# First depthwise tap folded into the projection weights, a third DMA product in every band, and a new order of work

## The chip, the cores and the metric

The kernel runs on one core of one Trainium2 chip. The metric is device time in microseconds of a whole execution, as the median of several runs. The profile covers one execution, from the first to the last instruction of the program (the span); the time of a run is some 20 us more than that.

Five engines run side by side and wait for each other only through semaphores: PE (matmuls), DVE (vector), ACT (activations and copies), POOL (GpSimd, which here also issues the adding DMAs) and SP (which issues plain DMAs). Sixteen DMA engines move data.

## The reference

The input x has 16 images of 128 channels, 96 x 96 pixels, in float32. One Restormer-like block is computed:

```python
x_hwc = x.transpose(0, 2, 3, 1)
xn1 = _layernorm(x_hwc, ln1_w, ln1_b)
x = x + _attention(xn1, wq, wk, wv, wp).transpose(0, 3, 1, 2)
xn2 = _layernorm(x.transpose(0, 2, 3, 1), ln2_w, ln2_b).transpose(0, 3, 1, 2)
h1 = einsum('bchw,oc->bohw', xn2, w_in)                 # 128 -> 512 channels
h2 = depthwise 3x3 convolution of h1 with w_dw, padding 1
h3 = gelu(h2)
x = x + einsum('bchw,oc->bohw', h3, w_out)              # 512 -> 128 channels
```

The attention is over channels (8 heads of 16), so that it needs one 128 x 128 Gram matrix per image. The change concerns the last four lines: the projection w_in, the nine taps of the depthwise convolution, the gelu and the projection back.

## The kernel before

**Tiling.** An image is 8 bands of 12 rows (1152 pixels); 16 images make 128 bands, called g. A band is 3 units of 4 rows (384 pixels). The 512 hidden channels are 4 chunks of 128, called n. A conv job is one chunk of one band, (g, n).

**Stages.** For each image `norm(i, False)` transposes x by PE (line 581), takes statistics on DVE (588), variance and power on POOL (595, 599), scales on ACT (626), forms the Gram matrix (640), transposes back (671) and copies to the padded buffer xn (677). `attention` makes one 128 x 128 matrix from the Gram matrix. `norm(i, True)` multiplies by that matrix (539), adds x (by a DMA that adds, 551) and normalizes again, into xn (675, 681).

**A conv job** (`conv_job`, line 838). PE multiplies by winT (line 856) and ACT copies the result from PSUM to h1 (861), with two rows kept from the band before (`halo`, 852). Then the nine taps are summed in h3, a buffer of 128 x 1152. Tap t is h1, shifted by t, times the channel's weight `dw[:, n, t]`. There are three ways for a tap:

- Tap 0 is a product on ACT that starts h3 (line 872 with h3 as the output).
- Taps 1 and 2 are products on ACT into buffers called pr (line 872 with pr as the output); a DMA adds the second to the first (line 880, pr<-pr), and another adds the first to h3 (line 880, h<-pr). In chunk 1 of two bands out of three (`THIRD`, line 26) tap 3 goes this way also. POOL issues these adding DMAs.
- The other taps are one DVE instruction each, h3 = h1 shifted x weight + h3 (line 876).

When all are in, ACT applies gelu to h3 in place (884), and `ffn_out` multiplies by woutT on PE (950), adds to x on DVE (957) and stores the band by SP (961).

In 66 of the 128 bands chunk 3 takes another way (`by_matmuls`, line 915): the weights of w_in and of each tap are multiplied together beforehand (`comp`), and nine matmuls per unit accumulate in PSUM (927); ACT applies gelu from there (933). So there are 446 conv jobs.

**What sets the order.** The kernel lists its operations with an engine, an assumed duration, a place and what it reads and writes (`Plan.op`, line 66). `Plan.order` (line 96) walks through assumed time; each free engine takes the ready operation with the lowest place. A place is the number of the job that it belongs to plus an offset per kind of operation, from the table `AT` (line 32). Buffers of some pools (`IN_TURN`) are given out in the order of place. The result is one fixed list for each engine. At run time an engine works through its own list in order and stalls at the first instruction whose inputs are not there. There are 10 h3 buffers, 5 pr buffers and 4 PSUM banks for the matmuls of this stage.

The weights are prepared once at the start (`weights`, line 401): they are transposed by PE and scaled by the second norm's weight w2 on the way out of PSUM.

Of the kernel before, what the change touches and what calls it, by code (L numbers as in the profile page):

```python
# [9 lines left out]
F32 = mybir.dt.float32  # L10
AF = mybir.ActivationFunctionType
ALU = mybir.AluOpType
# [6 lines left out]
BR = 12  # L19
# [2 lines left out]
PE_OF = 2  # L22
PE_LAST = (0, 1, 2, 4, 5, 7)
TINY = 1e-20
DMA_TAPS = (1, 2, 3)
THIRD, THIRD_OF, THIRD_CHUNK = (0, 1), 3, 1
PART, Z_PARTS = 24, 6
QT, QB = 4, 1
H_BANKS = 4
X1_BUFS, XB_BUFS, PR_BUFS, H3_BUFS, ZT_BUFS = 2, 6, 5, 10, 3  # L30
IN_TURN = ("tr", "h3", "pr", "xb", "x1")
AT = dict(
    weights=8.1, zeros=0.25, load_a=-21.3, forth_a=-15.05, stats_a=-18, variance_a=-18.05, power_a=-1.8,
    scaled_a=0.55, gram=-6.85, back_a=-25.85, place_a=-18.35, attention=-17.8, mix=-10.5, residual=4.7,
    mixed=-4.65, add_x=14, forth_b=-14.75, stats_b=-10.65, variance_b=-15.9, power_b=-13.85,
    shift_b=-25.75, scaled_b=3.95, back_b=-24.6, place_b=5.05, halo=9.05, hidden=0.85, kept=-0.9,
    product=-13.2, products=5.45, add_last=-13.7, tap=3.45, add_first=27.05, gelu=-5.15, conv=0.55,
    conv_gelu=-14.15, out=4.35, add=-4.2, store=7.05,
)
STEP = dict(scaled=0.3, hidden=0.1, products=0.5, tap=0.166, conv=1.6, conv_tap=0.03, out=0.8, out_part=0.05)  # L40
SLACK = 300
# [9 lines left out]
class Plan:  # L51
# [14 lines left out]
    def op(self, engine, ns, place, work, reads, writes, result, own=None, dma=0, two=False):  # L66

        k = len(self.ops)
        needs = {}
        for t in reads:
            if t in self.writer:
                needs[self.writer[t]] = True
        for t in writes:
            if t in self.writer:
                needs[self.writer[t]] = True
            for r in self.readers.get(t, ()):  # L80
                needs[r] = True
        for t in reads:
            self.readers.setdefault(t, []).append(k)
        new = []
        for t in writes:
            self.writer[t], self.readers[t] = k, []
            if t[0] in self.free and t[:2] not in self.users and t[:2] not in new:
                new.append(t[:2])
        for t in {t[:2]: None for t in (*reads, *writes)}:
            if t[0] in self.free:  # L90
                self.users.setdefault(t, []).append(k)
                needs[self.users[t][0]] = True
        needs.pop(k, None)
        self.ops.append((engine, ns, place, work, list(needs), new, result, own or result, dma, two))
# [111 lines left out]
def tile_restormer_block(  # L206
# [24 lines left out]
    nc = tc.nc  # L231
    B, C, H, W = x.shape
    P = 128
    HID = w_in.shape[0]
    NCH = HID // P
# [42 lines left out]
    wv_sb = const.tile([P, P], F32, name="wv_sb")  # L278
    nc.scalar.dma_start(out=wv_sb, in_=wv)
    dw = const.tile([P, NCH, 9], F32, name="dw")  # L280
    nc.scalar.dma_start(out=dw, in_=w_dw.rearrange("(n p) o kh kw -> p n (o kh kw)", p=P))

    wvb = const.tile([P, 1], F32, name="wvb")
# [59 lines left out]
    def at(kind, place):  # L343
        return place + AT[kind]
# [16 lines left out]
    def t_act(n, scalars=0):  # L361
        return 95 + 93 * scalars + 0.832 * n
# [7 lines left out]
    def dve(ns, p, f, r, w, two=False):  # L370
        op("DVE", ns, p, f, r, w, ns + 120 + SLACK, ns + 120, two=two)
# [7 lines left out]
    def act(ns, p, f, r, w):  # L379
        op("ACT", ns, p, f, r, w, ns + 150 + SLACK, ns + 150)  # L380
# [20 lines left out]
    def weights(p):  # L401
# [17 lines left out]
        def transposed(parts, kept, gives):  # L419

            key = ("weights", next(names))
            h = ("h", key)
            d = {}

            def forth():
                d["pt"] = bank(key)
                for k, part in enumerate(parts()):
                    nc.tensor.transpose(d["pt"][:, k * P : (k + 1) * P], part, ident)

            pe(440, at("weights", p), forth, mine, [h])  # L430
            dve(700, at("weights", p), lambda: kept(d["pt"]), [h], [("w", g) for g in gives] + mine[1:])
# [37 lines left out]
        def shifts():  # L469
# [4 lines left out]
            nc.vector.reciprocal(none, w2)  # L474
            nc.vector.tensor_mul(b2, b2, none)

        op("ACT", 400, at("load_a", p), loads, [], mine, T_WEIGHTS, dma=2 * T_MOVE)
        dve(400, at("weights", p), shifts, [], [("w", "in"), ("w", "conv"), ("w", "shift")])
        transposed(
            lambda: [v["wqk"][:, :P], v["wqk"][:, P:], v["wp"], wv_sb], keep_qkp, ["qk"]  # L480
# [3 lines left out]
        pc = ("h", ("weights", "centred"))  # L484
        pe(1000, at("weights", p), centred, [("w", "qk"), mine[1]], [pc])
        dve(800, at("weights", p), keep_centred, [pc], [("w", "qk")])
        transposed(
            lambda: [v["win"][:, n, :] for n in range(NCH)],
            lambda pt: nc.vector.tensor_scalar(winT.rearrange("p n c -> p (n c)"), pt, w2, None, ALU.mult), ["in"],
        )  # L490
        transposed(
# [341 lines left out]
    def h3_of(g, n):  # L833
        if (g, n) not in h3s:
            h3s[g, n] = h3p.tile([P, BR, W], F32, tag="h3", name=f"h3_{g}_{n}")
        return h3s[g, n]

    def conv_job(j, g, n):

        i, b = divmod(g, NB)  # L840
        kz, r0 = part_of(i, b * BR)
        xn = xns[kz]
        d = {}
        jn = (g, n)
        from_halo = n != PE_CHUNK and b > 0
        to_halo = n != PE_CHUNK and b < NB - 1
        h1_ = h1s[n]
        step = 4 if from_halo else 5
        chunks = [(k, min(k + step, BR + 2)) for k in range(2 if from_halo else 0, BR + 2, step)]

        def halo():
            nc.scalar.copy(window(h1_, 0, 2, 1), window(h1_, BR, 2, 1))

        def hidden(r, e):
            ph = d["ph", r] = bank((jn, r), (e - r) * W)
            nc.tensor.matmul(  # L856
                rows(ph), lhsT=winT[:, n, :], rhs=window(xn, r0 + r, e - r, 1), start=True, stop=True
            )

        def kept(r, e):  # L860
            nc.scalar.copy(window(h1_, r, e - r, 1), rows(d.pop(("ph", r))))  # L861

        def shifted(t):
            dy, dx = divmod(t, 3)
            return window(h1_, dy, BR, dx)

        def product(t):
            if t == 0:
                to = h3_of(g, n)
            else:  # L870
                to = d["pr", t] = prp.tile([P, BR, W], F32, tag="pr", name=f"pr_{g}_{n}_{t}")
            nc.scalar.activation(to, shifted(t), AF.Copy, scale=dw[:, n, t : t + 1])  # L872

        def tap(t):
            h3 = h3_of(g, n)
            nc.vector.scalar_tensor_tensor(h3, shifted(t), dw[:, n, t : t + 1], h3, ALU.mult, ALU.add)  # L876

        def add_products(t):
            to = d["pr", DMA_TAPS[0]] if t != DMA_TAPS[0] else h3_of(g, n)
            nc.gpsimd.dma_start(out=to, in_=d["pr", t], accum_op=ALU.add)  # L880

        def gelu(s0, s1):
            h3 = h3_of(g, n)[:, s0 * UR : s1 * UR, :]
            nc.scalar.activation(h3, h3, AF.Gelu)  # L884

        last = j == len(jobs) - 1
        third = n == THIRD_CHUNK and g % THIRD_OF in THIRD
        dma_taps = () if last else DMA_TAPS[: 3 if third else 2]
        left = [t for t in range(1, 9) if t not in dma_taps]
        h1 = [("h1", n, k) for k in range(4)]  # L890
        h3 = [("h3", jn, s) for s in range(UPB)]
        for k, (r, e) in enumerate(chunks):
            ph = ("h", (jn, r))
            jk, zs = j + STEP["hidden"] * k, z_units(kz, r0 + r, r0 + e)
            to = h1[k + 1 : k + 2] if r else h1[:2]
            pe(t_mm((e - r) * W), at("hidden", jk), lambda r=r, e=e: hidden(r, e), [*zs, ("w", "in")], [ph])
            act(t_copy((e - r) * W), at("kept", jk), lambda r=r, e=e: kept(r, e), [ph], to)
        act(t_act(BR * W, 1), at("product", j), lambda: product(0), h1, h3)
        for k, t in enumerate(dma_taps):
            jk = j + STEP["products"] * k  # L900
            act(t_act(BR * W, 1), at("products", jk), lambda t=t: product(t), h1, [("pr", (jn, t))])
        pr = [("pr", (jn, t)) for t in dma_taps]
        for k, t in enumerate(dma_taps[1:]):
            add(at("add_last", j), lambda t=t: add_products(t), [pr[1 + k]], [pr[0]])
        for k, t in enumerate(left):
            dve(t_dve(BR * W), at("tap", j + STEP["tap"] * k), lambda t=t: tap(t), h1, h3, True)
        if dma_taps:
            add(at("add_first", j), lambda: add_products(DMA_TAPS[0]), [pr[0]], h3)
        if to_halo:
            act(t_copy(2 * W), at("halo", j), halo, h1[3:], h1[:1])  # L910
        for s in range(0, UPB, 1 if last else UPB):
            e = s + 1 if last else UPB
            act(t_act((e - s) * UT), at("gelu", j), lambda s=s, e=e: gelu(s, e), [], h3[s:e])
# [121 lines left out]
```

## Time and profile before

| | before |
|---|---|
| time, median of 3 | 4262.72 us (4255.91 to 4265.92) |
| span of the profile | 4242.3 us |
| instructions | 52552 |
| POOL busy | 2403.9 us (57%) |
| DMA bytes | 802.87 MB, mean 189 GB/s |
| adds pr<-pr, h<-pr, to x (issues; us to landing) | 531; 6.8, 445; 7.0, 122; 7.5 |

A line of a group reads: line, engine, operation, output<-inputs, shape, count, then busy time in us and mean ns of one, then the engine's idle time just before them and what ended most of it. A record of an instruction can overlap the next one on the same engine, so that the busy time of a group (the time in which at least one of its instructions ran) can be below count times mean. PEld is the loading of weights into the PE, which overlaps matmuls. A matmul in float32 is two instructions.

Queue rows of the page, in words: the queue of adding DMAs (software_dynamic) moved 647.70 MB and took 80.5% of the time of the 16 DMA engines; the plain loads and stores (hardware_dynamic) moved 151.01 MB and took 9.8%.

### The profile page before, as it was taken

The numbers are of one execution on the slowest core, as the hardware profiler recorded it, in microseconds if no ns is written. First come the engines' busy times: TensorE is split into PE (matmuls) and PEld (weight loads), VectorE is DVE, ScalarE is ACT, GpSimd is POOL, SyncE is SP. The second block draws the span as 40 slices with busy tenths as digits, with TensorE's granted clock in tenths as the row PEclk, the third lists the DMA queues.
The fourth block names the chain that finished last, engine by engine and source line by source line (L and its number), as shares of the span: only waits on it lengthen the run. The fifth ranks groups of instructions, "written<-read, shape, count | busy, mean of one in ns | idle before, by whom it ended". The sixth has DMA issues, their size and how long they took to land.

```text
span 4242.3 us, 52552 instructions
## 1 busy us (share of the span) xinstructions
PE 4175.6 (98%) x17457; PEld 2667.1 (63%) x17457; DVE 4121.0 (97%) x4705; ACT 4080.1 (96%) x7374; POOL 2403.9 (57%) x2331
## 2 busy tenths in 40 slices
PE   8999999999999999999999999999999999999999
PEld 6566666666665666666666666666666666666565
DVE  6999999999999999999999999999999999999999
ACT  5999999999999999999999999999999999999996
POOL 4656556565665656655656565666655556465432
PEclk9999999999999999999999999999999999999999
DMA  2989899899998999899999989999989899998997
GB/s 81 188 179 203 187 199 205 187 203 189 192 193 188 195 192 198 186 191 199 191 207 190 194 190 185 204 191 193 207 179 202 188 198 198 182 201 180 185 188 161
DMA packets 197887, 802.87 MB, mean 189 GB/s; under 512 B 22896, under 2 KB 24304, under 8 KB 197616
## 3 DMA queue, kind: packets, MB, share of 16 engines
q0 software_dynamic: 158112, 647.70, 80.5%
q1 hardware_dynamic: 37152, 151.01, 9.8%
q8 instruction: 138, 2.26, 0.2%
q10 hardware_dynamic: 2352, 0.81, 0.1%
q14 instruction: 133, 1.09, 0.1%
HBM read 148.26 MB, written 75.50 MB: 53 GB/s over the span
## 4 chain that ended last, share of the span: by engine, by line
PE 49%; ACT 20%; DVE 13%; DMA 5%; issue 3%; POOL 1%; POOLq 0%; ACTq 0%; DVEq 0%
PE h L927 15%; PE h L950 11%; DVE h L876 11%; PE h L856 10%; ACT pr L872 5%; DMA h<-pr 3%; PE g L640 3%; PE h L539 3%; ACT h L861 3%; ACT h L884 2%; ACT h L872 2%; ACT zT L630 2%; PE pB_a L671 2%; PE pT_b L581 1%; PE pB_b L671 1%
## 5 line engine op out<-in xcount | busy, mean ns | idle before, releaser
L876 DVE SCALAR_TENSOR_TENSOR h<-h,dw,h 128x1152 f32<-128x1152 f32 x2592 | 3563.1, 1410 | 12.6 <-ACT h L872 9.3
L872 ACT ACTIVATE pr<-h,dw 128x1152 f32<-128x1152 f32 x976 | 1319.9, 1376 | 8.9 <-DMA pr<-pr 8.8
L927 PE MATMUL h<-xn,comp 128*128 128x384 f32 x3564 | 1268.1, 486 | 4.3 <-ACT h L861 2.6
L950 PE MATMUL h<-h,woutT 128*128 128x384 f32 x3072 | 1120.9, 488 | 12.2 <-ACT h L861 7.2
L856 PE MATMUL h<-xn,winT 128*128 128x384 f32 (+1 forms) x2676 | 1055.2, 501 | 10.7 <-ACT h L861 3.7
L927 PEld LDWEIGHTS h<-xn,comp 128*128 128x128 f32 x3564 | 648.1, 190 | 402.6 <-issue 14.1
L880 POOL DMA_DIRECT2D pr<-pr x531 | 493.0, 934 | 596.1 <-ACT pr L872 444.5
L950 PEld LDWEIGHTS h<-h,woutT 128*128 128x128 f32 x3072 | 558.2, 190 | 366.0 <-ACT h L861 17.5
L861 ACT COPY h<-h 128x384 f32<-128x384 f32 (+1 forms) x1338 | 722.2, 605 | 21.2 <-PE h L856 18.7
L880 POOL DMA_DIRECT2D h<-pr x445 | 425.2, 963 | 520.6 <-DVE h L876 183.2
L856 PEld LDWEIGHTS h<-xn,winT 128*128 128x128 f32 x2676 | 483.1, 190 | 320.6 <-issue 38.9
L872 ACT ACTIVATE h<-h,dw 128x1152 f32<-128x1152 f32 x446 | 603.8, 1361 | 1.8 <-PE h L950 0.2
L884 ACT ACTIVATE h<-h 128x1152 f32<-128x1152 f32 x448 | 565.7, 1263 | 34.4 <-DMA h<-pr 32.1
L599 POOL TENSOR_TENSOR rstd_b<-ve_b,mhalf 128x4 f32<-128x4 f32 x288 | 496.6, 1730 | 10.4
L599 POOL TENSOR_TENSOR rstd_a<-ve_a,mhalf 128x4 f32<-128x4 f32 x288 | 492.8, 1712 | 10.5 <-POOL ve_a L595 0.2
L630 ACT ACTIVATE zT<-pT_b,nb_b,rstd_b 128x128 f32<-128x128 f32 x1132 | 455.9, 572 | 4.5 <-DVE nb_b L603 4.5
L595 POOL TENSOR_SCALAR ve_b<-st_b 128x4 f32<-128x4 f32 x288 | 297.3, 1041 | 257.0 <-DVE st_b L588 253.9
L595 POOL TENSOR_SCALAR ve_a<-st_a 128x4 f32<-128x4 f32 x288 | 275.8, 958 | 265.7 <-DVE st_a L588 263.6
L626 ACT ACTIVATE zT<-pT_a,rstd_a 128x128 f32<-128x128 f32 x1080 | 339.3, 492 | 13.6 <-POOL rstd_a L599 13.4
L640 PE MATMUL g<-zT 128*128 128x129 f32 x2304 | 306.7, 276 | 0.0
L539 PE MATMUL h<-xn,mwT 128*128 128x384 f32 x768 | 284.0, 489 | 2.1 <-ACT zT L630 0.7
L640 PEld LDWEIGHTS g<-zT 128*128 128x128 f32 x2304 | 282.4, 192 | 2.5 <-issue 0.4
(165 smaller groups left out, 3713.2 us busy)
## 6 DMA issues: line engine op xcount, KB each, us to landing
pr<-pr POOLq DMA_DIRECT2D x531, 576.0 KB, 6.8
h<-pr POOLq DMA_DIRECT2D x445, 576.0 KB, 7.0
x<-in_x_dram SPq DMA_DIRECT2D x128, 576.0 KB, 6.2
out_dram<-x SPq DMA_DIRECT2D x127, 576.0 KB, 5.3
x<-in_x_dram POOLq DMA_DIRECT2D x122, 576.0 KB, 7.5
out_dram<-x SPq DMA_DIRECT2D x3, 192.0 KB, 1.9
weights<-in_L_conv_w_in_dram ACTq DMA_DIRECT2D x1, 256.0 KB, 11.3
weights<-in_L_conv_w_out_dram ACTq DMA_DIRECT2D x1, 256.0 KB, 12.2
```

The costliest lines, as they stand in the source:

```text
L595: nc.gpsimd.tensor_scalar(ve, d["mv"][:, :, 2], 1.0 / C, EPS, ALU.mult, ALU.add)
L599: nc.gpsimd.tensor_tensor(rstd, d["ve"], mhalf, ALU.pow)
L630: nc.scalar.activation(zT(q)[:, k, :P], d["pT", q][:, k, :], AF.Identity, bias=d["nb"][:, t : t + 1], scale=d["rstd"][:, t : t + 1],)
L640: nc.tensor.matmul(grams[i][:, : P + 1], lhsT=zt[:, :P], rhs=zt, start=(q == 0 and k == 0), stop=(q == NU * TPU // QT - 1 and k == QT - 1),)
L856: nc.tensor.matmul(rows(ph), lhsT=winT[:, n, :], rhs=window(xn, r0 + r, e - r, 1), start=True, stop=True)
L861: nc.scalar.copy(window(h1_, r, e - r, 1), rows(d.pop(("ph", r))))
L872: nc.scalar.activation(to, shifted(t), AF.Copy, scale=dw[:, n, t : t + 1])
L876: nc.vector.scalar_tensor_tensor(h3, shifted(t), dw[:, n, t : t + 1], h3, ALU.mult, ALU.add)
L880: nc.gpsimd.dma_start(out=to, in_=d["pr", t], accum_op=ALU.add)
L884: nc.scalar.activation(h3, h3, AF.Gelu)
L927: nc.tensor.matmul(d["pc"], lhsT=comp[:, t, :], rhs=window(xn, r0 + dy, UR, dx), start=(t == 0), stop=(t == 8),)
L950: nc.tensor.matmul(rows(d["po"]), lhsT=woutT[:, n, :], rhs=h3s[g, n][:, s * UR : (s + 1) * UR, :], start=(k == 0), stop=(k == NCH - 1),)
```

## The change

It has three parts.

1. **Tap 0's weight goes into the projection.** Before it is transposed, w_in is multiplied by tap 0's weight of each hidden channel (`unit`; a weight that is almost zero is replaced by a tiny one). Then h1 shifted is tap 0's product, and no instruction is needed for it. The other taps use `ratio`, their weight divided by tap 0's. The first tap on DVE reads h1 twice, once with its own shift and weight, once with shift 0, and writes h3.
2. **The third DMA product in chunk 1 of every band.** `THIRD` takes all three residues of g instead of two.
3. **A new table `AT`**, and so a new order on every engine.

```diff
+UNIT_MIN = 1e-18
-THIRD, THIRD_OF, THIRD_CHUNK = (0, 1), 3, 1
+THIRD, THIRD_OF, THIRD_CHUNK = (0, 1, 2), 3, 1
...
 AT = dict(
-    weights=8.1, zeros=0.25, load_a=-21.3, forth_a=-15.05, stats_a=-18, variance_a=-18.05, power_a=-1.8,
...
-    product=-13.2, products=5.45, add_last=-13.7, tap=3.45, add_first=27.05, gelu=-5.15, conv=0.55,
-    conv_gelu=-14.15, out=4.35, add=-4.2, store=7.05,
+    weights=86, zeros=34, load_a=-17.95, forth_a=-1.35, stats_a=-23.85, variance_a=50.15, power_a=-16.45,
...
+    scaled_b=98.5, back_b=-23.15, place_b=20.55, halo=21.65, hidden=1.35, kept=-79.55, products=8.4,
+    add_last=-64.4, tap=0.1, add_first=-14.5, gelu=-63.5, conv=1.15, conv_gelu=-1.85, out=4.9, add=-43.45,
+    store=47.1,
 )
...
+        def units():
+
+            w0 = dw[:, :, 0]
+            nc.vector.tensor_scalar(unit, w0, -1.0, None, ALU.mult)
+            nc.vector.tensor_tensor(unit, unit, w0, ALU.max)
+            nc.vector.tensor_scalar(unit, unit, UNIT_MIN, 3 * UNIT_MIN, ALU.is_lt, ALU.mult)
+            nc.vector.tensor_add(unit, unit, w0)
+            nc.vector.reciprocal(per_unit, unit)
+            for n in range(NCH):
+                nc.vector.tensor_scalar(ratio[:, n, :], dw[:, n, :], per_unit[:, n : n + 1], None, ALU.mult)
+
+        def unit_parts():
+            for n in range(NCH):
+                nc.vector.tensor_scalar(v["wt"][:, n, :], v["win"][:, n, :], unit[:, n : n + 1], None, ALU.mult)
...
         def product(t):
-            if t == 0:
-                to = h3_of(g, n)
-            else:
-                to = d["pr", t] = prp.tile([P, BR, W], F32, tag="pr", name=f"pr_{g}_{n}_{t}")
-            nc.scalar.activation(to, shifted(t), AF.Copy, scale=dw[:, n, t : t + 1])
+            to = d["pr", t] = prp.tile([P, BR, W], F32, tag="pr", name=f"pr_{g}_{n}_{t}")
+            nc.scalar.activation(to, shifted(t), AF.Copy, scale=ratio[:, n, t : t + 1])
 
         def tap(t):
             h3 = h3_of(g, n)
-            nc.vector.scalar_tensor_tensor(h3, shifted(t), dw[:, n, t : t + 1], h3, ALU.mult, ALU.add)
+            onto = shifted(0) if t == left[0] else h3
+            nc.vector.scalar_tensor_tensor(h3, shifted(t), ratio[:, n, t : t + 1], onto, ALU.mult, ALU.add)
...
-        act(t_act(BR * W, 1), at("product", j), lambda: product(0), h1, h3)
```

In `weights` the transposes of w_in read the multiplied copy `wt` in place of `win`, with `units` and `unit_parts` listed on DVE before them.

More of the change, by code (lines that the diff above doesn't have):

```diff
@@ L32 @@
 AT = dict(
-    weights=8.1, zeros=0.25, load_a=-21.3, forth_a=-15.05, stats_a=-18, variance_a=-18.05, power_a=-1.8,
-    scaled_a=0.55, gram=-6.85, back_a=-25.85, place_a=-18.35, attention=-17.8, mix=-10.5, residual=4.7,
-    mixed=-4.65, add_x=14, forth_b=-14.75, stats_b=-10.65, variance_b=-15.9, power_b=-13.85,
-    shift_b=-25.75, scaled_b=3.95, back_b=-24.6, place_b=5.05, halo=9.05, hidden=0.85, kept=-0.9,
-    product=-13.2, products=5.45, add_last=-13.7, tap=3.45, add_first=27.05, gelu=-5.15, conv=0.55,
-    conv_gelu=-14.15, out=4.35, add=-4.2, store=7.05,
+    weights=86, zeros=34, load_a=-17.95, forth_a=-1.35, stats_a=-23.85, variance_a=50.15, power_a=-16.45,
+    scaled_a=6.1, gram=-31.8, back_a=-145.85, place_a=68, attention=-19.55, mix=-17.6, residual=60.15,
+    mixed=-98.2, add_x=-22.85, forth_b=-2, stats_b=-5.55, variance_b=52.05, power_b=-11, shift_b=-76.95,
+    scaled_b=98.5, back_b=-23.15, place_b=20.55, halo=21.65, hidden=1.35, kept=-79.55, products=8.4,
+    add_last=-64.4, tap=0.1, add_first=-14.5, gelu=-63.5, conv=1.15, conv_gelu=-1.85, out=4.9, add=-43.45,
+    store=47.1,
 )
@@ L280, in tile_restormer_block @@
     dw = const.tile([P, NCH, 9], F32, name="dw")
+    ratio = const.tile([P, NCH, 9], F32, name="ratio")
+    unit = const.tile([P, NCH], F32, name="unit")
+    per_unit = const.tile([P, NCH], F32, name="per_unit")
     nc.scalar.dma_start(out=dw, in_=w_dw.rearrange("(n p) o kh kw -> p n (o kh kw)", p=P))
@@ L475, in shifts @@
             nc.vector.tensor_mul(b2, b2, none)
+        def units():
[10 more added lines that the diff above has]
+                nc.vector.tensor_scalar(v["wt"][:, n, :], v["win"][:, n, :], unit[:, n : n + 1], None, ALU.mult)
         op("ACT", 400, at("load_a", p), loads, [], mine, T_WEIGHTS, dma=2 * T_MOVE)
+        dve(1400, at("weights", p), units, [], [("w", "in")])
         dve(400, at("weights", p), shifts, [], [("w", "in"), ("w", "conv"), ("w", "shift")])
@@ L486, in weights @@
         dve(800, at("weights", p), keep_centred, [pc], [("w", "qk")])
+        dve(700, at("weights", p), unit_parts, [mine[0], ("w", "in")], [mine[1]])
         transposed(
-            lambda: [v["win"][:, n, :] for n in range(NCH)],
+            lambda: [v["wt"][:, n, :] for n in range(NCH)],
             lambda pt: nc.vector.tensor_scalar(winT.rearrange("p n c -> p (n c)"), pt, w2, None, ALU.mult), ["in"],
```

## The prediction

> **What bounds the kernel now.** I read the page's first part (busy time per engine) and then its slices:
>
> ```profile
> PE 4175.6 (98%) x17457; PEld 2667.1 (63%) x17457; DVE 4121.0 (97%) x4705; ACT 4080.1 (96%) x7374; POOL 2403.9 (57%) x2331
> ...
> DVE  6999999999999999999999999999999999999999
> ACT  5999999999999999999999999999999999999996
> ...
> DMA  2989899899998999899999989999989899998997
> ```
>
> Three engines are full at once, from the first tenth to the end. No stage has a single bound, so a saving on one engine alone need not show. The windows view (per stretch: length, then busy time and count for PE, PEld, DVE, ACT, POOL, then clock, DMA share, GB/s) gives start, middle and end:
>
> ```profile
> 0.00:106.00 106.00, 87.72 (x546) 69.72 (x547) 66.39 (x183) 53.21 (x134) 43.61 (x100) 0.95 0.27 81
> 106.00:4136.00 4030.00, 3985.46 (x16592) 2537.70 (x16591) 3958.57 (x4441) 3957.40 (x7146) 2338.61 (x2207) 1.00 0.93 193
> 4136.00:4243.00 107.00, 102.43 (x324) 59.70 (x322) 96.06 (x83) 69.51 (x97) 21.67 (x24) 1.00 0.76 160
> ```
>
> In the middle, 4030 us, DVE and ACT are both 98.2% busy and the DMA engines 0.93. The PE's 3985 us needs care, since matmuls overlap in the records. The timeline gives the true spacing:
>
> ```profile
> 2008.43 1.06 PE L640 MATMUL g<-zT 128*128 128x129 f32 x8
> ...
> 2009.66 0.81 PE L856 MATMUL h<-xn,winT 128*128 128x384 f32 x2
> ...
> 2013.86 0.60 PE L581 MATMUL pT_b<-ident,x 128*128 128x128 f32 x4
> ...
> 2020.47 4.68 PE L927 MATMUL h<-xn,comp 128*128 128x384 f32 x14
> ...
> 2023.33 4.07 DVE L876 SCALAR_TENSOR_TENSOR h<-h,dw,h 128x1152 f32<-128x1152 f32 x3
> ```
>
> A run of 14 wide matmuls takes 4.68 us and one of 2 takes 0.81: (4.68 - 0.81)/12 = 0.3225 us each. A run of 4 narrow ones takes 0.60, and three elsewhere 0.49: 0.11 each. By shape, the groups hold 9640 of 384 columns (3109 us), 440 of 480 columns (0.403 by proportion, 177 us) and 7377 narrower (811 us): 4098 us of real PE work. The groups of the first stretch (46, 16 and 484 of these shapes) make 75 us, those of the last (312 and 12) 102 us, so the middle holds 3921 us, 97.3% of 4030. It loses 109 us there, DVE and ACT 72 and 73. These are three almost equal loads. DMA, behind them, is not far off.
>
> The groups by line give what the change touches:
>
> ```profile
> L876 DVE SCALAR_TENSOR_TENSOR h<-h,dw,h 128x1152 f32<-128x1152 f32 x2592 | 3563.1, 1410 | 12.6 <-ACT h L872 9.3
> L872 ACT ACTIVATE pr<-h,dw 128x1152 f32<-128x1152 f32 x976 | 1319.9, 1376 | 8.9 <-DMA pr<-pr 8.8
> ...
> L872 ACT ACTIVATE h<-h,dw 128x1152 f32<-128x1152 f32 x446 | 603.8, 1361 | 1.8 <-PE h L950 0.2
> L884 ACT ACTIVATE h<-h 128x1152 f32<-128x1152 f32 x448 | 565.7, 1263 | 34.4 <-DMA h<-pr 32.1
> ```
>
> Taps (L876) are 86% of DVE. Products (L872) are 47% of ACT. The only DMA wait of note on an engine is the gelu's, 32.1 us in all.
>
> **What the Trainium skill says.** "Perfetto Trace Analysis", section "Identifying the Most-Contended Engine", says that matmul busy share is a poor measure; this trace agrees (98% busy, 96.6% by spacing: 4098/4242.3). The same page, "Optimizing Scalar/DVE Operations", says that an instruction's recorded latency overlaps the next one's start. Agreed: one tap is recorded at 1.41 us and three at 4.07, so each further tap costs (4.07 - 1.41)/2 = 1.33. "DMA: Bandwidth & Descriptors", "Issuing engines are not separate DMA queues", says that transfers from all issuers share 16 engines. The queue rows agree in kind: the adds' queue takes 80.5% and the plain one 9.8% of the same engines. "GPSIMD Engine Reference", "1. Specifications", says that GpSimd's SBUF interface contends with DVE instructions that have two SBUF inputs. The trace fits: the 4-element power takes 996 to 4668 ns. A first tap that reads h1 twice still has two SBUF inputs, so nothing changes here.
>
> **The change part by part.**
>
> Tap 0's product. 446 ACT instructions go. On the chain of waits one product advances ACT by 1.15 us (records of 1.36 overlap by the rest), so 446 x 1.15 = 513 us. The first remaining tap on DVE now reads h1 twice and writes h3 afresh. It has the same shape and two SBUF inputs, so I take the same 1.33 us. The trace has no tap with both inputs from h1. Bounds: the same as now, or 0.08 more (the record/spacing difference) on 446, which is 36 us; I take nothing, as both windows have the same layout. The tap no longer waits for product 0 (9.3 us in total) but for the last copy into h1 (L861), which product 0 waited for itself. Behind a waiting tap on DVE stand the statistics and the output adds (L957) that release PSUM banks to the PE. With a lighter ACT those copies come no later. The h3 buffer is taken at the first tap instead of at the product, so it is held for less time.
>
> Third product in every band. It was in g mod 3 = 0 or 1: 86 of 128 bands; now 128. So 42 taps leave DVE: 42 x 1.33 = 56 us. 42 products come to ACT: 42 x 1.15 = 48 us. POOL issues 42 more adds at 0.93, 39 us, on an engine that is 57% busy and is waited for little (nb_b 35 us). The DMA engines take them: the queue's 80.5% of 4242.3 is 3415 us over 1098 issues (531 + 445 + 122), or 3.11 us each, 131 us more in all.
>
> Preparation. Nine tiny DVE instructions of about 0.16 us and four of 0.29 (the rows of line 465 and of the attention's small operations): 3 us. They lie in the first 106 us, where DVE is idle for 40 and waits for the first x to be loaded and transposed. At most 3 us on the path, I take 0.
>
> The scale itself costs nothing: winT is made once, ratio takes dw's place, and matmuls, PSUM copies and halo are unchanged in number. PE work stays 4098 us.
>
> New order. It cannot be costed from instructions. The listed order of the changed kernel shows the same pattern: the first conv matmul comes some four listed rows later on PE than before, and the end still alternates the taps of the last two jobs and closes on three output adds. I take start and end as unchanged.
>
> Sums for the middle: ACT falls by 465 us of 3957, to about 87%. DVE goes from 3959 to 3903, PE stays at 3921, DMA goes from 0.93 x 4030 = 3748 to 3879. ACT leaves the race; DVE and PE remain, with DMA close behind.
>
> **How it can go.**
>
> A, likeliest: DVE keeps the fill that it has, 98.2%. The middle is 3903/0.982 = 3974, 56 us less. PE must then reach 3921/3974 = 98.7%. For: most waits of PE on others name ACT's copies (L861, L677, L630, L675), which get ACT's slack, and from 4030 on PE already runs nearly without loss. Against: PE has had 97.3% over the middle. Time 4262.7 - 56 = 4206.
>
> B, the PE keeps its losses: 97.3% again, so the middle stays 4030, plus 3 us of preparation at most: 4263. The PE waits also name output adds on DVE (L957), which remain queued behind taps of 1.41 us. Against: half of what it waits for is relieved.
>
> C, more than A: with ACT out of the race both others fill better, PE 99.1% and DVE 98.7%. The middle is 3921/0.991 = 3957, 73 less, and the stretch just after the start, where ACT and DVE were full while PE was not, gives perhaps 8: 4182. For: ACT's slack is 13%. Against: the fill of two engines together has not been that good over any long stretch.
>
> D, slower: the adds become the bound. A needs a DMA share of 3879/3974 = 97.6%; the old time needs 96.3%. If the queue can be kept only at 95%, the middle is 3879/0.95 = 4083, 53 more: 4316. For: the share is 0.93 now, the adds wait in POOL's order behind products and taps (444.5 and 183.2 us of waits), and late adds hold the gelu, so h3, so the PE's output matmuls. Against: windows of 53 us already show shares of 0.99 to 1.01 without DVE losing anything (530 to 583: DVE 53.00 of 53). Packets of two queues overlap, so the share is not a hard ceiling at 1; the gelu waited 32 us in all; and ACT's slack makes products earlier.
>
> **How the numbers follow.** A 0.55, C 0.18, B 0.17, D 0.10. The predicted time is A's, 4206. The range, 4172 to 4252, holds A and C and half way towards B (a middle gain of 10 us), and leaves out B at its full, D, and a start shorter by more than C's. Within A the terms move it little: the first taps' bound of 36 us would give 4242, inside. Chances: faster by over 0.2% (below 4254) is A and C and the part of B in which some of the loss goes, 0.86; the same 0.05; slower 0.09, nearly all D.
>
> **What would show it.** Right: 2550 taps at about 1410 ns, 1018 products on pr and none on h, 573 adds pr<-pr; ACT near 3600 busy, DVE near 4065, and DVE over 98% of the middle; the DMA share of the middle 0.96 or more with the gelu's DMA wait still under 60 us; PE losing some 50 us in the middle. Wrong: taps above 1410 (the doubled h1 read costs), a gelu wait in the hundreds (D), or DVE's fill down with waits on PE or POOL in its place (B).

## The result, and the profile after

| | before | after |
|---|---|---|
| time, median of 4 runs each | 4259.57 us (4255.91 to 4265.92) | 4200.59 us (4194.94 to 4202.23) |
| ratio | | 0.9861, 95% interval 0.9847 to 0.9875 |
| span of the profile | 4242.3 us | 4193.2 us |

The change makes the kernel 59 us faster by the timed runs, where 56.7 were predicted (4262.7 to 4206); the two profiled executions are 49 us apart. In the runs a time is 1.7 us above the span of the same execution. The 20 us that the section on the chip gives as the difference are between two executions of the kernel before, the profiled and the median one, and not a fixed cost. In the later sets of runs the kernel before took 4240.8 to 4242.7 us. So kernels are compared below by their ratio to the kernel before in the same set. Where a time is put beside an expectation, which was given on the scale of the first set, it is the ratio times 4259.57.

Busy time per engine, and three rows of the slices, from the page of the kernel after:

```profile
PE 4151.7 (99%) x17457; PEld 2684.0 (64%) x17457; DVE 4073.2 (97%) x4676; ACT 3682.0 (88%) x6970; POOL 2593.8 (62%) x2373
...
DVE  6999999999999999999999999999999999999998
ACT  4988989899899888999988899898998989889885
...
DMA  2999999999999999999999999999999999999997
```

ACT has left the group of full engines, and DVE and PE have not. The DMA row is at nine tenths throughout. The windows view of after (length, then busy time and count for PE, PEld, DVE, ACT and POOL, then clock, DMA share, GB/s), with the middle cut to the shorter span:

```profile
0.00:106.00 106.00, 89.63 (x547) 72.41 (x548) 67.84 (x196) 51.42 (x132) 41.19 (x98) 0.95 0.26 80
106.00:4086.00 3980.00, 3958.39 (x16582) 2550.76 (x16581) 3910.73 (x4400) 3570.32 (x6749) 2530.20 (x2250) 1.00 0.95 201
4086.00:4193.00 107.00, 103.64 (x330) 60.83 (x328) 94.61 (x82) 60.30 (x91) 22.45 (x25) 1.00 0.74 161
```

The middle is 3980 us where it was 4030; start and end are as long as before, so that the whole difference lies there. DVE fills 3910.7/3980 = 98.3% of it, as it did before (98.2%). The PE's work by spacing is again 4098 us, since the counts are the same. The first stretch holds 52 matmuls of 384 columns, 16 of 480 and 479 narrower, 76 us; the last 317 and 13, 104 us. That leaves 3918 us in the middle, 98.4% of it (97.3% before); the 98.9% that some expectations below give for it is too high. PE loses 62 us there instead of 109.

The groups that answer to those shown of before:

```profile
L895 DVE SCALAR_TENSOR_TENSOR h<-h,ratio,h 128x1152 f32<-128x1152 f32 x2104 | 2933.0, 1415 | 5.0
L890 ACT ACTIVATE pr<-h,ratio 128x1152 f32<-128x1152 f32 x1018 | 1304.2, 1290 | 21.8 <-DMA pr<-pr 20.3
...
L895 DVE SCALAR_TENSOR_TENSOR h<-h,ratio 128x1152 f32<-128x1152 f32 x446 | 630.1, 1419 | 11.5 <-ACT h L882 7.8
L903 ACT ACTIVATE h<-h 128x1152 f32<-128x1152 f32 x448 | 533.7, 1192 | 51.9 <-DMA h<-pr 48.0
```

2104 + 446 = 2550 taps, 1018 products into pr, none into h. The first tap of a job (the 446, with h1 on both sides) takes 1419 ns against 1415 for the others: reading h1 twice costs at most these 4 ns. The gelu waits for adds 48.0 us instead of 32.1. From the list of waits of after (who waits for whom: us in total, times, longest):

```profile
ACT h L882 <- PE h L877: 122.4, 249, 2.7
...
ACT h L903 <- DMA h<-pr: 48.0, 42, 6.4
...
DVE nb_b L624 <- POOL rstd_b L620: 38.3, 35, 2.0
...
DVE x L975 <- PE h L968: 6.8, 16, 2.9
```

ACT now waits for the PE. The longest wait of DVE is the one for the reciprocal deviation from POOL, as before (35.0).

### The profile page after: what moved, and what is told of

Its sections match the earlier page's. It is cut to its first block, busy times and chain, and to the rows that moved or that the text cites. A ratio compares the mean times of both kernels' runs of the same rounds, so it can differ in the third digit from the quotient of the medians.

```text
span 4193.2 us, 52283 instructions
## 1 busy us (share of the span) xinstructions
PE 4151.7 (99%) x17457; PEld 2684.0 (64%) x17457; DVE 4073.2 (97%) x4676; ACT 3682.0 (88%) x6970; POOL 2593.8 (62%) x2373
## 5 line engine op out<-in xcount | busy, mean ns | idle before, releaser
L895 DVE SCALAR_TENSOR_TENSOR h<-h,ratio,h 128x1152 f32<-128x1152 f32 x2104 | 2933.0, 1415 | 5.0
L890 ACT ACTIVATE pr<-h,ratio 128x1152 f32<-128x1152 f32 x1018 | 1304.2, 1290 | 21.8 <-DMA pr<-pr 20.3
L877 PE MATMUL h<-xn,winT 128*128 128x384 f32 (+1 forms) x2676 | 1048.4, 500 | 2.1 <-DVE x L975 1.1
L899 POOL DMA_DIRECT2D pr<-pr x573 | 545.7, 960 | 475.1 <-ACT pr L890 325.7
L882 ACT COPY h<-h 128x384 f32<-128x384 f32 (+1 forms) x1338 | 658.1, 521 | 139.7 <-PE h L877 122.4
L877 PEld LDWEIGHTS h<-xn,winT 128*128 128x128 f32 x2676 | 479.5, 190 | 290.9 <-issue 49.7
L895 DVE SCALAR_TENSOR_TENSOR h<-h,ratio 128x1152 f32<-128x1152 f32 x446 | 630.1, 1419 | 11.5 <-ACT h L882 7.8
L903 ACT ACTIVATE h<-h 128x1152 f32<-128x1152 f32 x448 | 533.7, 1192 | 51.9 <-DMA h<-pr 48.0
L616 POOL TENSOR_SCALAR ve_b<-st_b 128x4 f32<-128x4 f32 x288 | 364.3, 1265 | 310.8 <-DVE st_b L609 304.6
L620 POOL TENSOR_TENSOR rstd_b<-ve_b,mhalf 128x4 f32<-128x4 f32 x288 | 525.1, 1823 | 13.9
L616 POOL TENSOR_SCALAR ve_a<-st_a 128x4 f32<-128x4 f32 x288 | 323.9, 1125 | 292.2 <-DVE st_a L609 291.7
L647 ACT ACTIVATE zT<-pT_a,rstd_a 128x128 f32<-128x128 f32 x1080 | 314.7, 398 | 39.3 <-POOL rstd_a L620 38.4
```

What stands on the lines that cost most here:

```text
L616: nc.gpsimd.tensor_scalar(ve, d["mv"][:, :, 2], 1.0 / C, EPS, ALU.mult, ALU.add)
L620: nc.gpsimd.tensor_tensor(rstd, d["ve"], mhalf, ALU.pow)
L877: nc.tensor.matmul(rows(ph), lhsT=winT[:, n, :], rhs=window(xn, r0 + r, e - r, 1), start=True, stop=True)
L890: nc.scalar.activation(to, shifted(t), AF.Copy, scale=ratio[:, n, t : t + 1])
L895: nc.vector.scalar_tensor_tensor(h3, shifted(t), ratio[:, n, t : t + 1], onto, ALU.mult, ALU.add)
```

## The experiments

**One part at a time.** The change has three parts, so I made the mixtures. Each changes only the lines shown. The first keeps the fold, with the old `THIRD` and the old table, in which one entry had to be chosen anew, since a conv job now takes its h3 buffer later:

```diff
--- after
-THIRD, THIRD_OF, THIRD_CHUNK = (0, 1, 2), 3, 1
+THIRD, THIRD_OF, THIRD_CHUNK = (0, 1), 3, 1
-AT = dict(...)          # the new table
+AT = dict(...)          # the table of before, but
+    conv_gelu=2.5,      # -14.15 before
```

> The fold alone: the changed kernel with the old THIRD (86 bands) and the old table AT, save conv_gelu at 2.5 in place of -14.15 (h3 is now taken at the tap, 16.65 places later than by the product, and the h3 buffers are handed out by place). ACT loses 513 us of products, DVE keeps its 2592 taps, PE and DMA keep their work. My theory (DVE's taps set the end, PE just behind; ACT's relief by itself buys little): the middle stays DVE-bound, 4250 to 4265. Rival one (ACT's relief is what freed the three-way race): 4205 to 4225. Rival two (the new order brings the gain): about 4260, and then the fold with the old order and all thirds stays there too.

Measured: ratio 0.9971 (0.9960 to 0.9983), 4247 on the scale of the expectation, 12 us less than before. ACT fell to 86% busy, and the time hardly followed. That is nearest to my theory, a little better than its range, and far from the first rival, that ACT's relief had freed the three-way race.

The second, with the third product in every band as well (only the table is old, with conv_gelu=2.5 again):

> Fold and third product in every band, old table AT (conv_gelu at 2.5): the changed kernel without its new order. My theory (instruction counts decide): DVE has its 56 us less, so 4200 to 4220. Rival (the new order brings the gain): 4245 to 4265, with DVE and PE both below their fill of after (98.3% and 98.9% of the middle).

Measured: 1.0002 (0.9994 to 1.0011), no change at all. My theory fell here, and the rival's range, 4245 to 4265, held. All five engines have the instruction counts of after, and nothing of the gain is there. Its busy time over the span, its middle and its waits:

```profile
PE 4169.8 (98%) x17457; PEld 2682.1 (63%) x17457; DVE 4086.1 (96%) x4676; ACT 3684.8 (87%) x6970; POOL 2423.0 (57%) x2373
```

```profile
106.00:4086.00 3980.00, 3928.79 (x16409) 2521.86 (x16408) 3876.74 (x4352) 3530.52 (x6682) 2336.44 (x2224) 1.00 0.94 199
```

```profile
DVE h L895 <- ACT h L882: 31.5, 24, 3.5
DVE x L975 <- PE h L968: 19.6, 22, 3.4
DVE nb_b L624 <- POOL rstd_b L620: 18.5, 20, 2.0
```

In the same stretch of 3980 us DVE fills 3876.7, 97.4%, and 173 fewer matmuls have been issued than in after. ACT is at 88.7%, DMA at 0.94. DVE waits for ACT's copies into h1 (7.8 us in after) and for output sums from PE (6.8 in after).

Waits are not all of it. DVE is busy for 13 us longer than in after (4086.1 against 4073.2) with the same instructions. Its list sets 270 taps directly behind a tap on the same h3, where that of after has 143 and that of the first mixture 70, and such a tap starts some 0.12 us later than another (see the last section). That is 127 x 0.12 = 15 of the 50 us between the spans of this kernel and of after; most of the rest is DVE's longer idle time.

The third has the new order, but 86 thirds as before:

```diff
--- after
-THIRD, THIRD_OF, THIRD_CHUNK = (0, 1, 2), 3, 1
+THIRD, THIRD_OF, THIRD_CHUNK = (0, 1), 3, 1
```

> The changed kernel with the old THIRD (86 bands): 42 taps back on DVE, 42 products and adds fewer. My theory (DVE sets the end): 42 x 1.33 = 56 us more than after, 4245 to 4257. Rival (PE sets the end of after, DVE only looks full): at most 20 us more, 4200 to 4220. Rival (adds on the DMA engines limit after): no slower than after, 4190 to 4200.

Measured: 0.9972 (0.9962 to 0.9983), 4248. With the new order the 42 taps are worth 0.9972 - 0.9861 = 1.1%, 47 us, of the 56 that they take on DVE (42 products and adds move the other way). This is as my theory had it. Beside the pair before it, it shows that the two go together: 42 taps fewer save 47 us in the new order, and cost 13 us in the old one (1.0002 against 0.9971), where (270 - 70) x 0.12 = 24 us go to the additional pairs alone.

The fourth gives the kernel before the third product in every band, and the fifth gives it the new table. That table has no entry for tap 0's product, so it was given the place of the first tap, 0.1; no other place was tried:

```diff
--- before
-THIRD, THIRD_OF, THIRD_CHUNK = (0, 1), 3, 1
+THIRD, THIRD_OF, THIRD_CHUNK = (0, 1, 2), 3, 1
```

> The kernel before with the third product in every band, nothing else: DVE loses 56 us, ACT gains 48 us on 3957 of 4030 in the middle. My theory (three full engines, the fullest sets the end): ACT sets the end, 4005/0.985 = 4066 in the middle, so 4285 to 4310. Rival (DVE alone set the time of before): 4205 to 4220.

```diff
--- before
-AT = dict(...)          # the table of before
+AT = dict(...)          # the new table, with
+    product=0.1,
```

> The kernel before with the new table AT and nothing else (tap 0's product gets the place 0.1, where the first tap stands in the new table). All work of before stays: DVE 3959, ACT 3957, PE 3921 of 4030 us in the middle. My theory (the new order pays only together with ACT's slack and the shorter DVE): ratio to before 0.998 to 1.015. Rival (the new order is better by itself): below 0.995.

Measured: the thirds without the fold 1.0237 (1.0222 to 1.0253), 4360; the new order without fold and thirds 1.0669 (1.0653 to 1.0685). Both are slower as expected, and both by more than I gave: I had added up work, and the loss is in the order: in waits, and in pairs of taps on one h3 (330 and 281, against 89 before; some 29 and 23 us). From the waits of DVE in each of the two:

```profile
DVE h L876 <- ACT h L872: 61.0, 53, 5.0
DVE x L957 <- PE h L950: 33.2, 35, 2.4
```

```profile
DVE h L876 <- ACT h L872: 87.5, 52, 6.9
DVE st_b L588 <- PE pT_b L581: 77.4, 47, 6.5
```

Taps wait for tap 0's product; before had 9.3 us of that. In the second the statistics wait for transposes from PE as well. So the new order, as it was tried here, is no better by itself: it is 6.7% slower on the load of before. How much of that comes from the place 0.1 of tap 0's product, for which DVE waits 87.5 us, is open.

The eight mixtures, as far as they ran (ratio to before; the old order with the fold has conv_gelu=2.5, the new one without it product=0.1):

| | old order | new order |
|---|---|---|
| neither | 1 | 1.0669 |
| fold | 0.9971 | 0.9972 |
| third products | 1.0237 | not tried |
| fold and third products | 1.0002 | 0.9861 |

**What sets the end of after.** Four kernels keep after's order on every engine and leave work out of the computation, on one engine or on two: an operation keeps its place and its assumed time in the plan, and issues nothing.

```diff
--- after: less DVE
         def tap(t):
             h3 = h3_of(g, n)
+            if n == 0 and t == 8:
+                return
--- after: less PE (in by_matmuls)
         def product(t):
...
+            if t == 4:
+                return
             dy, dx = divmod(t, 3)
--- after: less DMA
         def add_products(t):
+            if t == DMA_TAPS[2]:
+                return
```

> After in its own order, with the last tap (t = 8) of chunk 0 left out of the computation in all 128 bands: DVE loses 128 x 1.33 = 170 us, all else stays. Theory A (DVE sets the end of after, PE next at 98.9% of the middle): the time falls only by what PE still loses, to 4165 to 4180. Rival (PE sets it already): under 10 us, 4192 to 4200. Rival (DMA adds set it): no change, 4198 to 4203.

> After in its own order, with the middle one of the nine composed matmuls left out of the computation in all 198 units of chunk 3: PE loses 396 x 0.3225 = 128 us, all else stays. Theory A (DVE sets the end): little, 4180 to 4198. Rival (PE sets it): 4080 to 4140.

> Both of the above left out: DVE -170 us, PE -128 us. Theory A (DVE and PE together are the wall): the middle falls to what ACT (3570 busy), DVE (3740), PE (3793) and DMA (0.95 of 3980, 3781) then allow, about 3850 to 3880, so 4075 to 4105, much more than the sum of the two single gains. Rival (DMA adds are the wall behind): 4150 or more.

> After in its own order, with the add of the third product left out of the computation (the product is still made): 128 adds or 128 x 3.05 = 390 us of the DMA engines' time go, POOL loses 128 issues. Theory A (DMA adds are hidden): 4190 to 4203. Rival D of the prediction (the adds have become the bound): below 4170.

| | taken away | ratio to before | us less than after |
|---|---|---|---|
| after | | 0.9861 (0.9847 to 0.9875) | |
| less DVE | 170 us of taps | 0.9826 (0.9810 to 0.9843) | 15 |
| less PE | 128 us of matmuls | 0.9797 (0.9783 to 0.9812) | 27 |
| less both | both | 0.9645 (0.9631 to 0.9660) | 92 |
| less DMA | 128 adds, 390 us, and their issues on POOL | 0.9846 (0.9831 to 0.9860) | 6 |

After itself was not in this set; its ratio comes from the first one. Each interval is some 6 us either way, and a difference of two some 9, so that the last row can't be told from none. DVE alone or PE alone gives little, 15 and 27 us. Both together give 92, more than twice the sum. Within the set itself the same shows: the matmuls are worth 77 us once the taps are gone (0.9826 to 0.9645), and the taps 65 once the matmuls are gone. Neither of the two is the bound: they are a double wall. The expectation for less DVE (4165 to 4180; measured 4185) and for less PE (4180 to 4198; measured 4173) both missed by a few us, in opposite ways. So PE may hold a little more of the wall, and DVE a little less, than "DVE sets the end"; the misses are about as large as the uncertainty. Less both was expected at 4075 to 4105, measured 4108. The same stretch of less both, whose span is 4091.4 us, so that this time most of the end lies in it:

```profile
106.00:4086.00 3980.00, 3946.59 (x16510) 2533.80 (x16509) 3840.40 (x4350) 3615.06 (x6839) 2464.68 (x2275) 1.00 0.97 206
```

Its DVE is 96.5% busy and DMA is at 0.97 (96.6% and 0.98 up to 3984 us, without the end), so DMA may well be next; that was not tried. For after, the adds are hidden: without 390 us of their time the kernel gains about 6 us, no more than the uncertainty, and rival D of the prediction is out.

**Which part of the order.** The old order lost time on copies into h1 that came late. The first guess was that they stand in ACT's list behind gelus and products that wait for adds, so one entry of the old table was changed:

```diff
--- fold and third products, old table
-    kept=-0.9,
+    kept=-79.55,
```

> Fold and all third products in the old order (ratio 1.000), with one entry changed: kept, the copies from PSUM into h1 (L882), goes from -0.9 to -79.55, its value in the new table, so that in ACT's list they stand ahead of products and gelus that may wait for adds. Theory K (in the old order the copies stand behind instructions that wait for adds, and taps and PE wait for the copies): DVE's wait for L882 falls from 31.5 us below 15 and the time to a ratio of 0.987 to 0.994. Rival (no single entry, the whole order): above 0.997.

Measured: 0.9997 (0.9988 to 1.0005). The theory fell: DVE's wait for the copies is still there, and no smaller.

```profile
DVE h L895 <- ACT h L882: 35.6, 28, 4.2
```

Then the table was cut in two, by kinds of operation. The first has the new entries from `halo` to `store` (conv jobs and output), the second the new entries for weights, norms and attention; the rest of each is old (in the second, conv_gelu=2.5).

> Fold and all third products; the new table only for the kinds of the conv jobs and the output (halo to store), the old one for weights, norms and attention. Theory (the places of products, adds, taps, gelus and copies carry the gain of the order): ratio to before 0.985 to 0.991. Rival (norm entries carry it): above 0.996.

> The reverse: the new table for weights, norms and attention, the old one for the kinds of the conv jobs and the output (conv_gelu at 2.5). Same theory: ratio to before 0.996 to 1.004. Rival (norm entries carry the gain): below 0.991.

Measured: new conv entries 0.9971 (0.9964 to 0.9978), new norm entries 0.9885 (0.9870 to 0.9900). It is the reverse of what I expected. The norm entries alone bring most of the gain, 1.2 of 1.4%, and those of products, adds, taps and gelus, around which the change turns, bring 0.3% alone. The middle and the waits with the new norm entries (line numbers are lower by 5 here, L890 is the tap, L877 the copy into h1, L970 the output sum, L963 the output matmul):

```profile
106.00:4086.00 3980.00, 3953.81 (x16574) 2550.14 (x16574) 3910.68 (x4397) 3575.39 (x6747) 2474.71 (x2249) 1.00 0.95 201
```

```profile
DVE h L890 <- ACT h L877: 20.2, 19, 4.4
...
DVE x L970 <- PE h L963: 5.1, 6, 2.9
```

DVE's fill is back at 3910.7, as in after. A small part of the difference arises at the start. In the first 212 us the old order (first line, fold and third products) has issued 975 matmuls and the new norm entries (second line) 986, and DVE has done 6 us more, of some 50 in all:

```profile
0.00:212.00 212.00, 183.10 (x975) 134.81 (x976) 166.32 (x310) 142.26 (x315) 110.56 (x164) 0.96 0.55 129
```

```profile
0.00:212.00 212.00, 189.51 (x986) 137.94 (x987) 172.69 (x311) 148.11 (x318) 107.35 (x162) 0.97 0.58 136
```

The number of matmuls by then is no measure of it: with the new conv entries it is 997, and DVE has done only 3 us more than in the old order. DVE's wait for copies into h1 is 11 us shorter than in the old order, and the pairs on one h3 are 194 instead of 270, some 9 us. What makes up the rest, and which of the norm entries does it, stays open. No kernel here separates them.

## Why the prediction was right, and where it was not

The predicted time was 4206 us by case A; measured were 4200.59. The sum over DVE's taps was right. The step that carries it to the time was not shown by the prediction, and to that extent the hit is luck: see "DVE keeps the fill" below. Point by point:

- **The bound.** "DVE and PE remain, with DMA close behind" held. The runs with work left out show it directly: 15 and 27 us singly, 92 together. That no single one of the three full engines of before set its time fits two runs: with 513 us less on ACT (fold alone) it gained 0.3%, and with 56 us less on DVE (third products alone) it lost 2.4%. It is not shown that ACT's 48 us more caused that loss of 100 us, since ACT is only 95% busy there and the order had changed too.
- **Tap 0's product at nothing on DVE.** Held: 1419 against 1415 ns. The 36 us named as its bound did not come.
- **42 taps at 1.33 us.** The size held. DVE's busy time fell by 4121.0 - 4073.2 = 48 us, of which the preparation takes some 3 back. The list of after also has 54 pairs on one h3 more than that of before, which do not overlap: 54 x (1.41 - 1.33), some 4 us. With the new order the 42 taps are worth 47 us of time.
- **ACT.** The sum had 465 us less; the busy time fell by 398, to 3682 and not to about 3600. The step that was mis-sized is the translation from spacing to busy time: the 1.15 us of a product is its spacing in a full queue, and its record is longer: 1.38 us before and still 1.29 after. An ACT that idles between instructions, as this one does for 12% of the span, may show more of each record as busy time. That this makes the 67 us is argued from the records, not shown.
- **DMA.** 131 us more were expected, and the queue's time rose from 3415 to 0.829 x 4193.2 = 3476, by 61. The mean time of the queue's packets fell from 345.6 to 338.8 ns (share x span x 16 / packets), so that all 1140 issues became a little cheaper, 3.05 us instead of 3.11. Hence 0.95 in the middle and not 0.976; the sign "0.96 or more" was missed. Why the packets are shorter was not tested.
- **"DVE keeps the fill that it has", on which case A rests.** True for the change as it is, 98.3%. It does not follow from the counts, as the prediction had it. With the same counts in the old order DVE's fill is 97.4%, PE gains nothing, and the time is that of before: case B. The prediction took the new order as something that "cannot be costed" and left it at nothing; it is the condition for the gain, and that the table was one with which the fill holds was luck as far as the prediction goes. It was right on the sum and too quick on this step.
- **Case C.** It did not come. Its sum has a slip: 3903/3957 is 98.6% for DVE, not 98.7%.
- **Start and end unchanged.** Held between before and after: 979 and 986 matmuls in the first 212 us. With fold and third products in the old order DVE has done 4 us less by then than before (166.3 against 170.3).

## What to carry to other kernels

When several engines are equally full, as here, removing work from one of them can buy little, and what removal from two of them buys can depend on the order of the instruction lists: sum up the work for the bound, and then ask separately whether the order lets that bound be reached. A table of priorities that suits one load need not suit another, so a change of load and a new table are to be judged together: either half alone can look worthless or harmful. To find out what bounds a kernel, leave out work on one engine, then on the next, then on both, with all orders kept: little singly and much together means a double wall.

## What was new about the hardware

A tap that directly follows a tap on the same h3 starts 1.45 us after it, and one that follows a tap on another h3 1.33 us. In the trace of after, with the h3 of each tap taken from the kernel's list, it is 143 pairs with a median of 1.453 us against 1011 with 1.328; in that of before 89 with 1.451 and 1081 with 1.329. From the timeline of after: the pair on one line takes 2.87 us for two taps of 1.42, with no overlap.

```profile
2013.96 1.42 DVE L895 SCALAR_TENSOR_TENSOR h<-h,ratio 128x1152 f32<-128x1152 f32 x1
2015.41 2.87 DVE L895 SCALAR_TENSOR_TENSOR h<-h,ratio,h 128x1152 f32<-128x1152 f32 x2
```

The first pair, 2015.41 - 2013.96 = 1.45, is of this kind too. In the records the second tap of each of these 143 pairs, and of the 89 of before, waits for a semaphore that DVE itself counts up, since it needs what the tap in front of it wrote. Many of the others wait for that semaphore too, but for an older instruction, and start after 1.33 us all the same. So the 1.45 us go with waiting for the end of the instruction directly in front, 1.41 us by its record, instead of overlapping it; whether the shared buffer would cost anything without that wait, no run here shows. Setting a tap of another job in between is worth 0.12 us a pair. After has 54 such pairs more than before, 6.5 us.

The mean granted clock of the TensorE, 0.998 over the span in before and after, was 0.990 with the third products alone and 0.985 with the new order alone, the two kernels in which PE idled most. That the idling is the cause was not tested.
